# Rows of negated maxima: block turns on VectorE and small transfers in place of products on TensorE

## The chip, the cores and the metric

The kernel runs on one core of a Trainium2 chip. The metric is device time in microseconds (us), the median of several runs. The engines are called as in the profile: PE (TensorE, products; PEld is its loading of weights), DVE (VectorE), ACT (ScalarE), POOL (GpSimd) and SP (SyncE, which here only issues transfers). Each engine works through its own queue in order, and the queues wait for each other by semaphores.

## The reference

Two layers on x of shape (2, 256, 64, 64), all float32. The first is attention with 8 heads of 32 channels over 4096 positions, with a projection and the input added; the second is a non-local block over 1024 pooled positions.

```python
# layer 0
qkv = einsum('oc,bchw->bohw', w_qkv, x); q, k, v = split(qkv, 3, axis=1)   # 8 heads x 32
scores = einsum('bhdi,bhdj->bhij', q, k) / sqrt(32)
attn = softmax(scores, axis=-1)
out = einsum('bhij,bhdj->bhdi', attn, v)
x = einsum('oc,bchw->bohw', w_proj, out) + x
# layer 1
g_x = maxpool2(conv1x1(x, g_w, g_b));  theta_x = conv1x1(x[:, :64], theta_w, theta_b)
phi_x = maxpool2(conv1x1(x[:, 64:], phi_w, phi_b))
f = softmax(einsum('bnc,bcm->bnm', theta_x, phi_x), axis=-1)
y = einsum('bnm,bmc->bnc', f, g_x)
x = batchnorm(conv1x1(y, W_w, W_b)) + x
```

Both softmaxes subtract the maximum of each row (of each query) before the exponential. The change is about how these maxima get from one place to another.

## The kernel before

**Tiling.** An image (b, two of them) has two groups of four heads (`QUAD`, numbered n = 0 to 3 over both images). For each group, `attend` runs over 8 blocks of 512 queries (i), and in each block over 32 steps of 128 keys (j). A step has four score products (`score`, L491: heads 2 and 3 as `pair` 1, then heads 0 and 1), two exponentials on ACT (L675), the products with v of the step before (`weigh`, L518) and their addition on DVE (L528). The sums of the exponentials, for the softmax's denominators, go to POOL (`add`, L555) and to accumulating transfers that POOL issues (L544). The scores of one block stay in PSUM and each step adds the difference of two chunks of keys to them (`turn_kd`, `mid_kd`, `kd`, `last_kd`).

**Maxima.** The maximum of every query over all 4096 keys must be known before its block begins. `maxima(n, i)` computes them one block ahead, as a generator that `advance(maxes)` moves on twice a step: products of q and k into PSUM (`product`, L330; the four heads lie in four groups of 32 rows of PE), for heads 0 and 1 a maximum straight from PSUM (L342), for heads 2 and 3 in pairs, with a difference and a relu on ACT (L350) and one DVE operation for both (L357). When a block's maxima are complete, DVE reduces `part` to `neg`, 128 x 16 numbers with the queries on the partitions (L434).

**Rows.** The exponential wants minus the maximum added to scores in which the queries lie along the free axis. So `negate` (L146) splits `neg` on POOL into three bfloat16 terms whose sum is exact enough (L150 to L154) and lays them into a 128 x 512 tile, of which most is zero. `rows()` then multiplies the tile with an identity matrix, four products of 128 x 128 (L159), which turns it over, and ACT copies the result from PSUM (L170). `subtract` (L500) begins each block's scores with the product of ones and these rows (L503). `make_rows` (L453) is called at every even step and makes a block's rows at the second call after they are ready.

**Lead.** Before the loop over blocks, `first_block` computes the maxima of the first block in 33 slots, with the items (k, v and q of the first group, `make`) between them. After it, four v items are made with two `advance` after each, so the maxima are ahead of the blocks by 8 calls, which is four steps. `LEAD = 4` stands in the code and isn't used.

**Items.** In the first three groups each of the first seven blocks makes one chunk of k and v of the next group at step 30 (block 6 also at step 11), and most blocks a q at step 11. They take their x from one buffer, which SP loads.

**Layer 1** (`non_local`) does the same with 8 row blocks of 512 queries for each image. `maxima1` computes maxima (`most`, L862; `neg`, L868) ahead by six groups of 128 queries, `step` the scores of two chunks of keys with their exponential (L1009), `weigh` the products with the values. Its PE instructions keep the program's order (`product1`, L712). `ready[i + 1]()` makes the next block's rows at the start of the second half of block i. `result` divides: the denominators go over DVE, two small transfers (L953, L954), DVE, two more (L961, L964), and then DVE multiplies and adds (L968, L969) and SP stores z (L970).

**SP's queue** holds, in one order fixed at build time, the loads of x, the small transfers of the denominators (layer 0: L617, L619, L635, L637), the key differences that are put away and fetched (L271 to L291), and the stores of the result.

## Time and profile before

| | |
|---|---|
| median of 3 runs | 3787.51 us (3785.46 to 3788.95) |
| the profiled execution: time / span | 3789.17 us / 3787.1 us |
| granted PE clock | 0.998 |
| first block's subtraction (L503) starts | 90.5 us |
| layer 0 of image 0 / image 1, from that subtraction to the last block's end, about | 90 to 1690 us / 1949 to 3522 us |
| period of a block with k and v at its end / in the last group | 99.64 us / 96.13 us |
| period of the first block of the last group | 112.33 us |
| L159: products in layer 0 / layer 1, busy | 128, 12.5 us / 64, 6.2 us |
| L170: copies in layer 0 / layer 1, busy | 32, 19.1 us / 16, 9.4 us |

Busy time is what an engine spends on instructions; a line's idle time is how long its engine stood still just before it, with what ended the wait. The order of time lists a start, a duration, the engine (PE, DVE, SPq for SP's queue), the line and operation, the tiles as output<-input, the shape and how many were merged. The long period in the last group has one cause: DVE waits 12.8 us for weights of layer 1 that land late (L763, then L767), and PE waits for DVE.

### The profile page before, as it was taken

Reading aid. Unit: us, or ns where it says so; the run is one execution under the profiler, and the core shown is the slowest. Engines: PE = TensorE matmul, PEld = TensorE weight load, DVE = VectorE, ACT = ScalarE, POOL = GpSimd, SP = SyncE. Lnnn points to the kernel's source line nnn. Section 1 sums busy time; section 2 is a strip of 40 time slices with the busy share of each in tenths; the row PEclk is TensorE's granted clock in tenths of the full one; section 3 lists DMA queues with packets and bytes.
Section 4 is the critical chain, followed back from the end, with each engine's and each line's share of the span. In section 5 each row is a group of like instructions: output and inputs, shape, how many; then the busy total and the mean of one; then the engine's idle time right before and its main releaser. Section 6 shows DMA issues by size and latency. Waiting matters only on the chain.

```text
span 3787.1 us, 69847 instructions
## 1 busy us (share of the span) xinstructions
PE 3759.5 (99%) x27186; PEld 1250.3 (33%) x27186; DVE 2981.3 (79%) x5841; ACT 2701.0 (71%) x3383; POOL 3077.8 (81%) x1944
## 2 busy tenths in 40 slices
PE   9999999999999999999999999999989999999999
PEld 4323333333333333334433333333222223222343
DVE  5888888888888888884468888888878888895444
ACT  5888788778888878771247887887868888887222
POOL 1889999899999999892458999999989999997244
PEclk9999999999999999999999999999999999999999
DMA  1788888889888888892128888888888888889501
GB/s 59 151 171 172 175 171 175 172 169 195 174 172 171 173 173 177 179 192 43 29 68 165 173 175 181 172 182 172 173 169 175 174 173 173 174 170 186 100 18 45
DMA packets 136028, 578.56 MB, mean 153 GB/s; under 512 B 37904, under 2 KB 42000, under 8 KB 74512
## 3 DMA queue, kind: packets, MB, share of 16 engines
q0 software_dynamic: 73184, 509.64, 67.9%
q1 hardware_dynamic: 61824, 64.20, 5.7%
q8 instruction: 212, 3.47, 0.4%
q14 instruction: 120, 0.98, 0.1%
q10 hardware_dynamic: 688, 0.27, 0.0%
HBM read 59.09 MB, written 12.69 MB: 19 GB/s over the span
## 4 chain that ended last, share of the span: by engine, by line
PE 97%; DMA 1%; DVE 1%; ACT 0%; issue 0%; POOL 0%; SPq 0%; ACTq 0%; POOLq 0%; DVEq 0%
PE ps L330 29%; PE w L518 26%; PE s L491 23%; PE y L712 6%; PE f L712 3%; PE q L206 2%; PE v L194 2%; PE proj L712 1%; PE k L206 1%; PE g L712 1%; PE tp L712 1%; DMA r<-flat 0%; DMA flat<-r 0%; PE s L503 0%; PE wg L712 0%
## 5 line engine op out<-in xcount | busy, mean ns | idle before, releaser
L555 POOL TENSOR_TENSOR p<-p,p 128x1024 f32<-128x1024 f32 x945 | 2357.7, 2495 | 279.5 <-ACT p L675 262.1
L675 ACT ACTIVATE p<-s 128x1024 f32<-128x1024 f32 x2048 | 2101.1, 1028 | 582.3 <-PE s L491 574.6
L330 PE MATMUL ps<-k,q 32*128 32x512 f32 x6080 | 2037.7, 625 | 2.8 <-DVE part L342 1.2
L342 DVE TENSOR_REDUCE part<-ps 128x1 f32<-128x512 f32 x1984 | 1278.5, 686 | 369.7 <-PE s L491 343.8
L518 PE MATMUL w<-p,v 128*32 128x512 f32 x8192 | 1080.6, 604 | 1.2 <-ACT p L675 0.8
L330 PEld LDWEIGHTS ps<-k,q 32*128 32x128 f32 x6080 | 607.1, 183 | 805.5 <-DVE part L342 696.4
L491 PE MATMUL s<-q,mid_kd 32*128 32x512 f32 x3072 | 749.8, 614 | 0.0
L357 DVE CUSTOM_DVE_ANT_0 ps<-ps,over 128x512 f32<-128x512 f32 x1056 | 727.7, 692 | 26.7 <-PE ps L330 13.5
L528 DVE TENSOR_TENSOR y<-y,w 128x512 f32<-128x512 f32 x938 | 645.0, 688 | 98.4 <-PE w L518 97.2
L350 ACT ACTIVATE over<-ps 128x512 f32<-128x512 f32 x992 | 588.0, 593 | 16.2 <-PE ps L330 16.0
L330 PE MATMUL ps<-kd,q 32*128 32x512 f32 x1056 | 523.7, 592 | 12.2 <-DVE part L357 11.8
L491 PE MATMUL s<-q,kd 32*128 32x512 f32 x2048 | 507.8, 618 | 0.3 <-ACT p L675 0.3
L491 PE MATMUL s<-q,last_kd 32*128 32x512 f32 x2048 | 504.6, 614 | 1.2 <-ACT p L675 1.2
L330 PE MATMUL ps<-last_kd,q 32*128 32x512 f32 x960 | 472.5, 589 | 0.0
L518 PEld LDWEIGHTS w<-p,v 128*32 128x32 f32 x8192 | 166.7, 108 | 771.0 <-DVE part L342 708.7
L544 POOL DMA_DIRECT2D p<-p x448 | 394.1, 880 | 7.1 <-ACT p L675 4.5
L491 PEld LDWEIGHTS s<-q,mid_kd 32*128 32x128 f32 x3072 | 247.6, 183 | 189.5 <-ACT p L675 181.5
L712 PE MATMUL y<-p,kv 128*128 128x512 f32 x512 | 229.7, 599 | 0.0
L491 PEld LDWEIGHTS s<-q,kd 32*128 32x128 f32 x2048 | 166.0, 184 | 131.6 <-ACT p L675 128.9
L491 PEld LDWEIGHTS s<-q,last_kd 32*128 32x128 f32 x2048 | 167.2, 183 | 124.5 <-ACT p L675 108.0
L862 DVE TENSOR_REDUCE most<-f 128x1 f32<-128x512 f32 x128 | 79.5, 683 | 143.1 <-PE f L712 142.7
L886 POOL TENSOR_TENSOR sums<-sums,p 128x512 f32<-128x512 f32 x96 | 128.0, 1334 | 77.7 <-ACT p L1009 72.9
(136 smaller groups left out, 2738.0 us busy)
## 6 DMA issues: line engine op xcount, KB each, us to landing
p<-p POOLq DMA_DIRECT2D x478, 1024.0 KB, 7.8
x_q<-in_x_dram SPq DMA_DIRECT2D x30, 512.0 KB, 6.7
x_k<-in_x_dram SPq DMA_DIRECT2D x24, 512.0 KB, 5.9
y<-in_x_dram POOLq DMA_DIRECT2D x16, 512.0 KB, 6.3
r<-flat SPq DMA_DIRECT2D x120, 64.0 KB, 5.6
out_dram<-z SPq DMA_DIRECT2D x14, 512.0 KB, 2.8
x<-in_x_dram SPq DMA_DIRECT2D x7, 512.0 KB, 7.0
r<-flat SPq DMA_DIRECT2D x12, 256.0 KB, 3.5
```

What stands on the lines that cost most here:

```text
L330: nc.tensor.matmul(ps, q[n, i][bass.ts(h, D), bass.ts(g, P)], keys[bass.ts(h, D), :], start=True, stop=True,)
L342: reduced = nc.vector.tensor_reduce(part[:, g, h, j : j + 1], ps, AX.X, ALU.max)
L350: cut = nc.scalar.activation(over, ps, AF.Relu)
L357: reduced = nc.vector.tensor_tensor_reduce(out=ps, in0=ps, in1=over, scale=1.0, scalar=LEAST, op0=ALU.add, op1=ALU.max, accum_out=part[:, ...
L491: nc.tensor.matmul(s[:, t, :], kj[bass.ts(h, D), :], q[blk.n, blk.i][bass.ts(h, D), :], start=False, stop=True, skip_group_check=j > 0,)
L518: nc.tensor.matmul(w[bass.ts(h, D), :], v[blk.n][:, keys(one), h, :], p[h // 2][:, h % 2, :], start=at == 0, stop=at == len(steps) - 1,)
L528: summed = nc.vector.tensor_add(blk.num, blk.num, w)
L544: sent = nc.gpsimd.dma_start(out=blk.sums[n], in_=two, accum_op=ALU.add)
L555: added = nc.gpsimd.tensor_add(blk.sums[0], blk.sums[0], p[0])
L675: nc.scalar.activation(p[pair], s, AF.Exp, scale=scale)
L712: last1 = tc.keep_in_program_order(nc.tensor.matmul(*args, **kw))
L886: nc.gpsimd.tensor_add(acc[i][NC], acc[i][NC], p[:, j, :])
```

## The change

The identity matrix and the products with it go. The three terms of `neg` are laid into a narrower tile, 128 x 64, in such an order that turning each 32 x 32 block over puts the numbers of one query group along a row. DVE turns the blocks in one operation (`transpose`). Four transfers store the used rows into DRAM (`flat4`), in an order in which each of the 12 rows (three terms of four heads) is contiguous, and four more load them, three rows each, into a constant tile with zeros elsewhere (`kept`, one for each layer). All eight are issued by SP, and the loads wait for the stores.

The maxima are six steps ahead in place of four (`LEAD = 6`): four more `advance` calls stand before the loop. The rows are made at step 26 of each block, behind that step's addition on DVE (`summed`). The addition of step 25's exponentials on POOL (`late`) is issued behind the splits (`split`). `fetch` issues the load of x for step 30's items at step 22. Before the loop, one more v item stands among the slots, each item is made in two parts with an `advance` between, and the last three v items use the scores' PSUM buffers (`wide`).

In layer 1 the first rows are made after the values of block 6, the others in the second half of the block before, behind the latest maxima on DVE (`reduced1`).

```diff
-    ident = work.tile([P, P], F32, tag="r", name="ident", bufs=1)
-    make_identity(nc, ident)
-    ident_b = const.tile([P, P], BF16, name="ident_b")
-    nc.vector.tensor_copy(ident_b, ident)
...
-    t = const.tile([P, NB // P, QH, D], BF16, name="terms")
-    nc.gpsimd.memset(t, 0.0)
+    TERMS, BLOCKS = 3, NB // P // 2
+    terms = const.tile([P, BLOCKS, D], BF16, name="terms")
+    nc.gpsimd.memset(terms, 0.0)
+    kept = [const.tile([P, NB], BF16, name=f"rows{layer}") for layer in range(2)]
+    for t in kept:
+        nc.gpsimd.memset(t, 0.0)
 
     def negate(name, neg, layer=0):
...
-        nc.gpsimd.tensor_copy(t[:, :, :, 0], neg)
-        nc.gpsimd.tensor_sub(rest, neg, t[:, :, :, 0])
-        nc.gpsimd.tensor_copy(t[:, :, :, 1], rest)
-        nc.gpsimd.tensor_sub(rest, rest, t[:, :, :, 1])
-        nc.gpsimd.tensor_copy(t[:, :, :, 2], rest)
-
-        def rows():
-            pt = scratch(f"pt_{name}")
-            for j in range(NB // P):
-                nc.tensor.matmul(
-                    pt[:, bass.ts(j, P)],
-                    t[:, j].rearrange("p h d -> p (h d)"),
-                    ident_b,
-                    start=True,
-                    stop=True,
+        nonlocal split
+        at = [four(terms[:, :, a * QH * BLOCKS : (a + 1) * QH * BLOCKS]) for a in range(TERMS)]
+        neg = neg.rearrange("p (i l) h -> p l h i", l=BLOCKS)
...
+        nc.gpsimd.tensor_copy(at[0], neg)
+        nc.gpsimd.tensor_sub(rest, neg, at[0])
+        nc.gpsimd.tensor_copy(at[1], rest)
+        nc.gpsimd.tensor_sub(rest, rest, at[1])
+        split = nc.gpsimd.tensor_copy(at[2], rest)
+
+        def rows(behind=None):
+            to = kept[layer]
+            turned = work.tile([P, BLOCKS, D], BF16, tag="turned", name=f"turned_{name}", bufs=1)
+            with tc.issue_after(behind.ins) if behind else ExitStack():
+                nc.vector.transpose(
+                    turned.rearrange("p l c -> p (l c)"), terms.rearrange("p l c -> p (l c)")
                 )
-            if layer == 0:
-                to = work.tile([P, NB], BF16, tag="rows", name=f"rows_{name}", bufs=1)
-            else:
-                to = work.tile([P, 2, NB], BF16, tag="over", name=f"rows_{name}")[:, 0, :]
-            nc.scalar.copy(to, pt)
+            used = TERMS * QH * BLOCKS
+            flat = spare.tile([used, BLOCKS, P // D, D], BF16, tag="flat4", name=f"flat4_{name}")
+            for a in range(P // D):
+                nc.sync.dma_start(out=flat[:, :, a, :], in_=turned[a * D : a * D + used])
+            those = flat.rearrange("(t h i) l a c -> t h (i l a c)", t=TERMS, h=QH)
+            for h in range(QH):
+                nc.sync.dma_start(out=to[h * D : h * D + TERMS], in_=those[:, h])
             return to
...
-        pq = scratch(name)
+        pq = scores(name)[:, 0, :] if wide else scratch(name)
...
                             if pair == 1:
                                 advance(maxes)
+                                if j == NJ - LEAD:
+                                    with tc.issue_after(split.ins):
+                                        add(*late)
                             score(s, pair, blk, j)
...
-                    add(blk, j, p, two)
+                    if j == NJ - LEAD:
+                        make_rows(summed)
+                    if j == NJ - LEAD - 1:
+                        late = blk, j, p, two
+                    else:
+                        add(blk, j, p, two)
...
-                    if j % 2 == 0:
-                        make_rows()
+                    if j == NJ - 10:
+                        for item in present(items.get(NJ - 2, ())):
+                            fetch(*item)
...
         for i in range(NI):
             values(i)
+            if i == NI - 2:
+                rows = ready[0](reduced1[0])
...
-                if u > 0 and i + 1 < NI:
-                    with tc.issue_after(last1.ins):
-                        rows = ready[i + 1]()
                 two = [step(i, u)]
-                if NB // P * i + u + LEAD1 < NI * NB // P:
-                    advance(maxes1, 2)
-                elif waiting:
+                more = NB // P * i + u + LEAD1 < NI * NB // P
+                for a in range(2):
+                    if more:
+                        advance(maxes1)
+                    if u > 0 and i + 1 < NI and a == 0:
+                        rows = ready[i + 1](reduced1[0])
+                if not more and waiting:
...
-    LEAD = 4
+    LEAD = 6
...
+    items.append(("v", NI - 4))
     for n, (what, i) in enumerate(items):
-        advance(make(what, 0, i), 3)
-        to = slots * (n + 1) // len(items)
-        advance(maxes, to - gone)
-        gone = to
-    for i in range(NI - 4, NI):
-        advance(make("v", 0, i), 3)
-        advance(maxes, 2)
-        if i < NI - 2:
-            make_rows()
+        item = make(what, 0, i)
+        advance(item)
+        if n > 0:
+            advance(maxes)
+            gone += 1
+        advance(item, 2)
+        to = (slots - 1) * (n + 1) // (len(items) - 1) if n < len(items) - 1 else slots + 1
+        advance(maxes, to - 1 - gone)
+        gone = to - 1
+    for i in range(NI - 3, NI):
+        advance(make("v", 0, i, True), 3)
+        if i == NI - 2:
+            make_rows(reduced)
+        advance(maxes, 3)
+    advance(maxes, 3)
```

In the order in which the changed program stands on SP, the four loads of a block's rows in layer 0 follow straight on its four stores; in layer 1 the store of z (L970 before, L986 after) stands between them for row blocks 3 to 6 of each image, and for row block 2 the first small transfer of a result.

More of the change, by code (lines that the diff above doesn't have):

```diff
@@ L7 @@
 from concourse._compat import with_exitstack
-from concourse.masks import make_identity
 F32 = mybir.dt.float32
@@ L138, in keep_bn_rows @@
             )
-    t = const.tile([P, NB // P, QH, D], BF16, name="terms")
-    nc.gpsimd.memset(t, 0.0)
-    def negate(name, neg, layer=0):
-        rest = work.tile([P, NB // P, QH], F32, tag="rest", name=f"rest_{name}")
-        nc.gpsimd.tensor_copy(t[:, :, :, 0], neg)
-        nc.gpsimd.tensor_sub(rest, neg, t[:, :, :, 0])
-        nc.gpsimd.tensor_copy(t[:, :, :, 1], rest)
-        nc.gpsimd.tensor_sub(rest, rest, t[:, :, :, 1])
-        nc.gpsimd.tensor_copy(t[:, :, :, 2], rest)
-        def rows():
-            pt = scratch(f"pt_{name}")
-            for j in range(NB // P):
-                nc.tensor.matmul(
-                    pt[:, bass.ts(j, P)],
-                    t[:, j].rearrange("p h d -> p (h d)"),
-                    ident_b,
-                    start=True,
-                    stop=True,
-                )
-            if layer == 0:
-                to = work.tile([P, NB], BF16, tag="rows", name=f"rows_{name}", bufs=1)
-            else:
-                to = work.tile([P, 2, NB], BF16, tag="over", name=f"rows_{name}")[:, 0, :]
-            nc.scalar.copy(to, pt)
+    TERMS, BLOCKS = 3, NB // P // 2
@@ new lines, in conv_attention, with four @@
+    terms = const.tile([P, BLOCKS, D], BF16, name="terms")
[3 more added lines that the diff above has]
+        nc.gpsimd.memset(t, 0.0)
+    def negate(name, neg, layer=0):
+        def four(ap):
+            return ap.rearrange("p l (h i) -> p l h i", i=BLOCKS)
+        nonlocal split
+        at = [four(terms[:, :, a * QH * BLOCKS : (a + 1) * QH * BLOCKS]) for a in range(TERMS)]
+        neg = neg.rearrange("p (i l) h -> p l h i", l=BLOCKS)
+        rest = work.tile([P, BLOCKS, QH * BLOCKS], F32, tag="rest", name=f"rest_{name}")
+        rest = four(rest)
+        nc.gpsimd.tensor_copy(at[0], neg)
[9 more added lines that the diff above has]
+                    turned.rearrange("p l c -> p (l c)"), terms.rearrange("p l c -> p (l c)")
+                )
+            used = TERMS * QH * BLOCKS
[5 more added lines that the diff above has]
+                nc.sync.dma_start(out=to[h * D : h * D + TERMS], in_=those[:, h])
@@ L171, in rows @@
             return to
         return rows
+    split = None
     QUAD = [(b, qd) for b in range(B) for qd in range(QUADS)]
@@ L178, in conv_attention, with fetch @@
     held = {}
-    def make(what, n, i):
-        b, qd = QUAD[n]
+    def fetch(what, n, i):
+        b = QUAD[n][0]
         if (b, i) not in held:
@@ L185, in make @@
             held[b, i] = load_x(b, i, xs.tile([P, NC, NB], F32, tag="x", name=name))
+    def make(what, n, i, wide=False):
+        b, qd = QUAD[n]
+        fetch(what, n, i)
         xc = held[b, i]
         name = f"{what}_{b}_{qd}_{i}"
-        pq = scratch(name)
+        pq = scores(name)[:, 0, :] if wide else scratch(name)
         if what == "v":
@@ L449, in advance, with make_rows @@
             next(steps, None)
-    seen = set()
-    def make_rows():
+    def make_rows(behind=None):
         for i, r in enumerate(rows):
             if callable(r):
-                if i in seen:
-                    rows[i] = r()
-                seen.add(i)
+                rows[i] = r(behind)
     def attend(b, y):
@@ L796, in non_local @@
         nc.gpsimd.tensor_sub(dphi, phi[:, 2 * P :], phi[:, : M - 2 * P])
+        reduced1 = [None]
         def values(i):
@@ L809, in values @@
                     )
-                nc.vector.tensor_reduce(
+                reduced1[0] = nc.vector.tensor_reduce(
                     g[:, o, small].rearrange("p (r w) -> p r w", w=WW // 2),
@@ L833, in w_values @@
                 nc.vector.tensor_add(wg[:, 2 * t + j, :], a[:, bass.ts(j, C)], shift_row)
-        ready, reduced1 = [], [None]
+        ready = []
         LEAD1 = NB // P + 2
@@ L1019, in non_local @@
                 w_values(i // 2 - 1)
-        with tc.issue_after(last1.ins):
-            rows = ready[0]()
         for i in range(NI):
             for u in range(0, last + 1, 2):
-                if u > 0 and i + 1 < NI:
-                    with tc.issue_after(last1.ins):
-                        rows = ready[i + 1]()
                 two = [step(i, u)]
-                if NB // P * i + u + LEAD1 < NI * NB // P:
-                    advance(maxes1, 2)
-                elif waiting:
+                more = NB // P * i + u + LEAD1 < NI * NB // P
[5 more added lines that the diff above has]
+                if not more and waiting:
                     weigh(*waiting.pop(0))
```

## The prediction

> **What bounds the kernel now.** I read the page's busy times and its chain first, then the groups by form, then the order of time around one place of each stage that the change touches.

> ```profile
> PE 3759.5 (99%) x27186; PEld 1250.3 (33%) x27186; DVE 2981.3 (79%) x5841; ACT 2701.0 (71%) x3383; POOL 3077.8 (81%) x1944
> PE 97%; DMA 1%; DVE 1%; ACT 0%; issue 0%; POOL 0%; SPq 0%; ACTq 0%; POOLq 0%; DVEq 0%
> ```

> TensorE (PE) holds 97% of the chain, so a microsecond off PE's queue counts in full, and so does one that PE waits. A busy share with modelled ends doesn't prove this, so I looked at the pace. Here is the end of a block of layer 0 (last head group, image 1), PE's rows and the copy on ACT:

> ```profile
> 3239.29 1.07 PE L518 MATMUL w<-p,v 128*32 128x512 f32 x8
> 3242.22 1.06 PE L518 MATMUL w<-p,v 128*32 128x512 f32 x8
> 3243.22 0.40 PE L159 MATMUL pt<-ident_b,terms 128*128 128x128 bf16 x4
> 3243.84 0.61 ACT L170 CAST rows<-pt 128x512 bf16<-128x512 f32 x1
> 3245.55 1.07 PE L518 MATMUL w<-p,v 128*32 128x512 f32 x8
> 3246.55 0.39 PE L503 MATMUL s<-rows,ones_b 32*128 32x512 bf16 x2
> ```

> From one `w` to the next a step takes 2.93 us, in this block after block; the step that holds the four L159 products takes 3.33. So the old way costs PE 0.40 us a block. The L170 copy is beside it: ACT idles before most of its work.

> VectorE (DVE) works 2 x 0.645 + 0.69 + 0.14 + 0.69 = 2.81 us of a step's 2.93 (L342, L357 with its read, L528), so it has little room. The block period (99.64 us with new k and v, 96.13 in the last head group) varies by at most 0.25 in the blocks between: there PE waits for nobody.

> **What is removed.** Layer 0: L159 in 32 rows, one of them ahead of the loop: 31 x 0.40 = -12.4 us. Layer 1: in the order of time the four products start at 1824.18 and the next work at 1824.50: 16 x 0.32 = -5.1. Before row 1 of each image PE waits 0.86 us for POOL's last split (L154): 2 x 0.86 = -1.7, as the splits leave PE's queue. ACT's 48 copies and the identity's building were hidden: nothing.

> **What is added on DVE and POOL.** 48 transposes of 128x64 bf16. Nearest is L634, 64x32 f32, 196 ns; bounds 0.16 (a small DVE operation, L131) and 0.44 (L605). At 0.2 us a block it fits in what DVE has free, 0.1 us a step and gaps of some 4 us at the k and v items; if that cover went it would be 48 x 0.2 = 10 us. The transpose must not wait for POOL: the splits take 1.8 us (L150 to L154) and stand now before the addition of p25 instead of behind that of p27. In the trace POOL ends the addition of p26 0.1 to 0.7 us before the L434 reduction ends, so two steps earlier it is ready likewise; the splits end 1.9 us after the reduction, the transpose comes a step later, 2.65 us after it. It waits for nothing, with 0.7 to spare. POOL gives up some 0.7 us a block to the wait for L434 and gets it back at its idle time of 1.7 to 4.6 us at each block's start.

> **What is added on SP: a chain of two hops.** Eight transfers a row: four into DRAM, a wait for their landing, four back into `kept`. They are on the path only if they land after PE wants them. The rows that price them:

> ```profile
> 3224.59 4.12 SPq L637 DMA_DIRECT2D r<-flat  x4
> flat<-r SPq DMA_DIRECT2D x42, 8.0 KB, 4.8
> r<-flat SPq DMA_DIRECT2D x120, 64.0 KB, 5.6
> r<-flat SPq DMA_DIRECT2D x12, 8.0 KB, 1.6
> ```

> The first line is the nearest: four in a row on SP, into few partitions, under layer 0's load. Their issues start at 0, 0.4, 1.6 and 2.9 us. At the start of the program seven loads of x go out in a row at 0.46 each; these are my two ends, 1.35 and 2.9 us to the last issue. Landing in layer 0: L635 3.6 at least, 5.1 median; L637 2.9 and 5.6. I take 4.4 us for each hop and the slow issue: transpose at 2.9 us behind the reduction's end, last store issued at 5.8, landed 10.2, last load issued 13.1, landed 17.5. Quickest: 2.9 + 1.35 + 3.6 + 1.35 + 2.9 = 12.1. Slowest, with medians: 19.4.

> PE's need: the reduction's end to L503 is 14.60 us now in the 21 blocks with k and v at the end, 11.10 at the three changes of head group and in six blocks of the last, 9.47 before the last block. Two steps of lead add 5.86 (5.2 before the last block, whose steps run at 2.39 and 2.83), less 0.40: 20.1, 16.6 and 14.3. So at 17.5 nothing waits in 21 blocks; 6 x 0.9 = 5.4 us in the last head group; 3.2 at the last block; at two changes of group (the third is covered by layer 1) `turn_kd` and `mid_kd`, 448 KB, go out just ahead on the same queue, an estimated 2 us more: 2 x 3 = 6. Sum +15 us, ends 0 and +33. What stands behind the rows on SP (`mid_kd`, `last_kd`, the next x) is issued some 6 us later and needed 11 us or more after the block's start: nothing.

> [...]

> **Layer 1** is where I expect the loss. The second half of row block 3, image 0:

> ```profile
> 1824.50 1.13 PE L712 MATMUL f<-theta,kv 64*128 64x512 f32 x4
> 1828.94 2.80 DVE L968 TENSOR_TENSOR z<-z,r 128x512 f32<-128x512 f32 x2
> 1831.66 2.35 DVE L969 TENSOR_TENSOR z<-z,y 128x512 f32<-128x512 f32 x2
> 1834.03 0.40 SPq L970 DMA_DIRECT2D out_dram<-z  x1
> 1834.65 0.33 SPq L953 DMA_DIRECT2D flat<-r  x1
> 1836.16 0.38 PE L712 MATMUL f<-rows_l,ones_b 64*128 64x512 bf16 x2
> ```

> Count from T = 1824.50. The transpose follows the first two `most` reductions (T+3.5). In the changed program's order SP then has the four stores, and for rows 3 to 6 of each image the store of z *before* the four loads. That store waits for L969: T+9.5 now, 9.7 with the transpose. The loads follow 0.62 us behind it (as L953 does), from 10.4 to 11.7, and land at 1.6 us at 13.3; PE wants them at 11.66. So PE waits 1.7 us with the quick issue, 4.0 with the slow one; I take 2.2, nearer to the quick end, since here SP's queue is almost empty and the nearest landing is 1.6. 8 x 2.2 = +17.6 (11.6 to 32). Behind the loads stands L953 of the next result, about 2 us later; its r still lands before z needs it. Rows 1, 2 and 7 have no such store ahead: stores land T+7.2, loads T+10.2, no wait (1.6 us each by the slow issue, +10 in the upper end).

> **Ahead of the loop.** Two more steps of maxima (1.9 us each between the v items at 85.6) come before the loop; at the end two steps run without products, 0.3 us less each: +3.2. The items in halves: DVE is starved behind each whole item.

> ```profile
> 24.28 0.70 DVE L357 CUSTOM_DVE_ANT_0 ps<-ps,over 128x512 f32<-128x512 f32 x1 [1.54 <-ACT k L220]
> 30.23 0.70 DVE L357 CUSTOM_DVE_ANT_0 ps<-ps,over 128x512 f32<-128x512 f32 x1 [1.31 <-PE ps L330]
> ```

> An item is 1.9 us of PE; cut in two, each piece starves DVE by at most 1.4 - 0.95 = 0.45, so 0.5 of 1.4 us is won an item: 13 x 0.4 = -5 (0 to -13: no gain, or DVE never dry, when PE's own work there becomes the bound). Together -2. The x load brought forward only keeps it ahead of the rows on SP.

> **Sum**, against the profiled span of 3787.1 us (that run 3789.2; median of the runs 3787.5): -12.4 - 6.8 - 2 + 15 + 17.6 = +11.4. On the median: 3799 us.

> **Rivals.**
> - *The rows are in time (faster).* If both hops land at L635's and L637's least times with quick issues, layer 0 waits nowhere, layer 1 only its 1.7: -12.4 - 6.8 - 2 + 0 + 13.6 = -7.6; with twice the gain of the halves -13: 3775. For it: L635's and L637's bytes are more than these rows have. Against: 4 issues at 1.2 us are the rule for L637. It decides from a chain under 14.3 us in layer 0.
> - *Even.* Chain at 16.5 us, 4 us of waits in layer 0, 14 in layer 1: -3, 3785.
> - *SP's slow issue everywhere (slower still).* Slow ends in both layers: -12.4 - 6.8 + 25 + 40 - 2 = +44: 3831. For it: L758 to L763 take 1.1 to 1.35 each too. Against: layer 1's queue is idle.

> **Chances.** Forecast 0.42 (own range 3789 to 3814); in time 0.26; even 0.16; slow issue 0.16. The low end is the second case's better gain with some more, 3770; the high end leaves out half of the last: 3828. Faster by over 0.2% (7.6 us, about what the runs can tell from no change) 0.27; within 0.23 (the even case and the forecast's lower edge); slower 0.50.

> **What would show it.** No L159 in the groups; steps of 2.93 us to the block's end; waits of PE before the subtraction put down to a DMA, none in blocks with k and v, 1 to 3 us in the last head group; in layer 1, PE idle before the `rows` product for rows 3 to 6, and there the loads issued right behind L986's store. It is wrong if four issues on SP in layer 0 end within 1.5 us, if PE waits in blocks with k and v (chain over 20 us), or if the DVE transpose waits for POOL and PE's step with it.

## The result, and the profile after

The changed kernel takes 3813.56 us (median of four runs, 3808.93 to 3817.24), the kernel before 3787.02 in the same series: a ratio of 1.0071, with a 95% interval of 1.0057 to 1.0084. It is slower by about 26.5 us. The profiled execution took 3816.07 us with a span of 3814.3, so its comparison with the span before (3787.1) has 27.2 us to explain.

The page of the changed kernel, its busy times and its chain:

```profile
PE 3768.9 (99%) x26994; PEld 1244.3 (33%) x26994; DVE 2992.6 (78%) x5888; ACT 2679.1 (70%) x3335; POOL 3079.5 (81%) x1944
PE 89%; DMA 3%; POOL 3%; issue 2%; DVE 2%; ACT 1%; SPq 1%; POOLq 0%; DVEq 0%; ACTq 0%
```

PE issues 192 products fewer and is still "busy" 9 us longer, in part because it runs part of the time at a lower clock (a mean of 0.994, before 0.998; below). The chain says more: PE held 97% of it and now holds 89%. PE waits for others, for POOL and for transfers above all.

The order of time at the end of a block of the last head group (image 1, the same block as was shown of before):

```profile
3248.32 0.28 DVE L444 TENSOR_REDUCE neg<-part 128x16 f32<-128x128 f32 x1
3251.24 0.24 DVE L166 STREAM_TRANSPOSE turned<-terms 128x64 bf16<-128x64 bf16 x1
3251.51 4.83 SPq L172 DMA_DIRECT2D flat<-turned  x4
3255.36 1.06 PE L523 MATMUL w<-p,v 128*32 128x512 f32 x8
3258.29 1.06 PE L523 MATMUL w<-p,v 128*32 128x512 f32 x8
3258.97 3.58 SPq L175 DMA_DIRECT2D rows<-flat  x4
3261.22 1.07 PE L523 MATMUL w<-p,v 128*32 128x512 f32 x8
3264.14 1.07 PE L523 MATMUL w<-p,v 128*32 128x512 f32 x8
3265.14 0.39 PE L508 MATMUL s<-rows,ones_b 32*128 32x512 bf16 x2
```

The products of L159 are gone, every step takes 2.93 us to the block's end, and the subtraction (L508, once L503) follows the last `w` after 1.00 us, as it did: here the rows come in time. An undisturbed block takes 99.29 us instead of 99.64. So this part of the change works, and the loss is elsewhere. The stretches from one block's first subtraction to the next, from PE's start times in both traces, show where:

```
stretch                                before    after   after - before
start of the program to block 0         90.49    92.19    +1.70
block 7  (last of head group 0)         96.22   103.23    +7.01
block 8  (first of head group 1)       101.15   104.65    +3.50
block 15 to layer 1's first rows       182.67   187.63    +4.96
layer 1, image 0, to block 16          174.02   176.84    +2.82
block 23 (last of head group 2)         96.40   102.49    +6.09
block 30                                92.85    95.11    +2.26
block 31 to layer 1's first rows       171.36   175.33    +3.97
layer 1, image 1, to the last product  173.52   176.20    +2.68
the other 26 blocks together                              -7.8
```

The three stretches at the ends of head groups 0, 1 and 2 hold 18.1 of the 27.2 us, and no step of the prediction has them. In the order of time there, the changed kernel:

```profile
824.96 2.48 POOL L246 TENSOR_TENSOR first_kd<-k 128x512 f32<-128x512 f32 x2
826.27 1.22 PE L340 MATMUL ps<-first_kd,q 32*128 32x512 f32 x1 [2.94 <-POOL first_kd L246]
827.28 1.06 PE L340 MATMUL ps<-first_kd,q 32*128 32x512 f32 x1
```

and the kernel before:

```profile
824.77 2.50 POOL L236 TENSOR_TENSOR first_kd<-k 128x512 f32<-128x512 f32 x2
828.42 0.60 PE L330 MATMUL ps<-first_kd,q 32*128 32x512 f32 x1
```

POOL makes `first_kd`, the key differences that the next head group's maxima read, at step 8 of the last block (`before_all`), as before. Its first half was ready at 826.0 and wanted at 828.4. With maxima six steps ahead PE wants it two steps, 5.86 us, sooner. The 2.4 us to spare become a gap of 3.5 us between two starts of PE, 2.94 of them idle. The busy times and the clock around it (columns: stretch, its length, busy time and count of each engine, granted PE clock, share of the DMA engines, GB/s), the changed kernel:

```profile
811.00:822.70 11.70, 11.70 (x86) 4.00 (x80) 8.20 (x17) 8.39 (x12) 11.62 (x8) 1.00 0.64 130
822.70:826.30 3.60, 0.66 (x6) 0.03 (x2) 1.09 (x2) 0.93 (x1) 3.60 (x3) 0.96 0.81 164
826.30:832.00 5.70, 5.70 (x20) 1.54 (x24) 1.80 (x4) 1.51 (x2) 3.88 (x3) 0.50 0.63 128
```

and the kernel before in the last of these stretches:

```profile
826.30:832.00 5.70, 5.70 (x52) 1.76 (x48) 5.70 (x13) 4.65 (x7) 5.62 (x4) 1.00 0.68 138
```

In the 5.7 us after the wait PE starts 20 products where it started 52: the granted clock is 0.50. The wait is paid for about twice, once as idle time and once as products at half the clock.

### The profile page after: what moved, and what is told of

It reads as the page before. It is cut to its first block, busy times and chain, and to the rows that moved or that the text cites. A ratio compares the mean times of both kernels' runs of the same rounds, so it can differ in the third digit from the quotient of the medians.

```text
span 3814.3 us, 70045 instructions
## 1 busy us (share of the span) xinstructions
PE 3768.9 (99%) x26994; PEld 1244.3 (33%) x26994; DVE 2992.6 (78%) x5888; ACT 2679.1 (70%) x3335; POOL 3079.5 (81%) x1944
## 4 chain that ended last, share of the span: by engine, by line
PE 89%; DMA 3%; POOL 3%; issue 2%; DVE 2%; ACT 1%; SPq 1%; POOLq 0%; DVEq 0%; ACTq 0%
PE ps L340 27%; PE w L523 24%; PE s L496 21%; PE y L726 4%; PE f L726 3%; DMA p<-p 2%; POOL p L560 2%; PE proj L726 1%; PE k L216 1%; PE q L216 1%; PE g L726 1%; PE v L204 1%; PE tp L726 1%; DVE z L984 0%; DMA rows<-flat_l 0%
## 5 line engine op out<-in xcount | busy, mean ns | idle before, releaser
L340 PE MATMUL ps<-kd,q 32*128 32x512 f32 x1056 | 525.3, 593 | 11.6 <-DVE part L367 10.6
L1025 ACT ACTIVATE p<-f 128x1024 f32<-128x1024 f32 x64 | 65.5, 1023 | 263.7 <-PE f L726 263.7
```

The costliest lines, as they stand in the source:

```text
L340: nc.tensor.matmul(ps, q[n, i][bass.ts(h, D), bass.ts(g, P)], keys[bass.ts(h, D), :], start=True, stop=True,)
```

## The experiments

Twelve kernels ran, each against the kernel before on the same chip. Ratios are to that kernel (its medians were 3786.7 to 3787.5), with 95% intervals.

**1. The wait for `first_kd`.** POOL's work and the q item that stands ahead of it are moved two steps forward, by as much as the maxima moved.

```diff
-        return {7: [("q", n + 1, 1)]}
+        return {5: [("q", n + 1, 1)]}
...
-                        if (i, j) == (NI - 1, 8) and blk.n + 1 < len(QUAD):
+                        if (i, j) == (NI - 1, 6) and blk.n + 1 < len(QUAD):
```

> The changed kernel with only this altered: in the last block of a head group the q item stands at step 5 instead of 7, and the differences of the next group's keys (`first_kd`, on POOL) are made at step 6 instead of 8. Theory (the lead of six steps brings the products that read `first_kd` two steps forward, while POOL still makes it at step 8): the three gaps of PE at 822.7, 1630.1 and 2697.2 (3.1 to 3.5 us each) go, and with them the 5.7 us at a granted clock of 0.50 behind each (some 2.9 us each): 3 x 6.3 = 19 us less, 3795 (3791 to 3799), and block 7 falls from 103.2 to about 97. Rival (PE stalls there because the rows' transfers slow POOL's accumulating DMAs, and `first_kd` is only what the wait is put down to): the gaps stay or move by a step, 3808 or more.

3798.16 us, ratio 1.0027 (1.0017 to 1.0037): 15.4 us less than the changed kernel. All three gaps (3.1 to 3.5 us between two starts of PE) are gone, block 7 takes 96.62, block 23 96.21, block 15's stretch 182.17. In this kernel's order of time and busy times:

```profile
820.90 2.74 POOL L246 TENSOR_TENSOR first_kd<-k 128x512 f32<-128x512 f32 x2
824.10 0.66 PE L340 MATMUL ps<-first_kd,q 32*128 32x512 f32 x1
826.30:832.00 5.70, 5.70 (x48) 1.62 (x48) 5.70 (x11) 4.59 (x7) 5.62 (x4) 1.00 0.95 191
```

The theory holds and the rival falls. The three stretches give back 18.3 us; the profiled run of this kernel loses 2.2 of that in block 0, where it shows a granted clock of 0.50 from 91.3 to 98.1 us, behind the short gaps ahead of the loop, and the changed kernel's profiled run doesn't.

**2. Is it the lead or the rows' transfers?** The kernel before with the lead alone: PE still turns the rows, no new transfer.

```diff
-    LEAD = 4
+    LEAD = 6
...
         advance(make("v", 0, i), 3)
-        advance(maxes, 2)
+        advance(maxes, 3)
```

> The kernel before with only the lead changed: maxima six steps ahead instead of four (three steps behind each of the last four v items instead of two), the rows still turned by PE, no new transfers. Theory (the lead alone brings the wait for `first_kd`): the same three gaps of PE of 3.1 to 3.5 us in blocks 7, 15 and 23, which then take some 102.5, 362 and 102.5 us; with the two later steps ahead of the loop 3787.5 + 18 + 4 = 3810 (3803 to 3814). Rival (the gaps come from the rows' transfers): blocks 7, 15 and 23 as before (96.2, 356.7, 96.4), 3791. Also looked at: block 8 and block 31, which became 3.5 and 6.7 us longer. If POOL's earlier splits or the lead are their cause, they are as long here; if the rows' transfers on SP are, block 8 is 101 here and block 31 345.

3813.75 us, ratio 1.0068 (1.0055 to 1.008): the lead alone costs as much as the whole change. Block 7 takes 102.77, block 15's stretch 189.18, block 23 101.50, with the same wait:

```profile
831.66 2.49 POOL L236 TENSOR_TENSOR first_kd<-k 128x512 f32<-128x512 f32 x2
832.98 1.22 PE L330 MATMUL ps<-first_kd,q 32*128 32x512 f32 x1 [2.51 <-POOL first_kd L236]
```

Block 8 is 101.21 here, as before, so what happens there comes with the rest of the change, not with the lead. Block 31's stretch is 174.82, nearly the 175.33 of the changed kernel, with the lead alone. And block 0 starts at 98.4 us: ahead of the loop the lead costs 7.9 us, not the 3.2 of the prediction.

**3. The halves.** The changed kernel with whole items ahead of the loop.

```diff
-        item = make(what, 0, i)
-        advance(item)
+        advance(make(what, 0, i), 3)
         if n > 0:
             advance(maxes)
             gone += 1
-        advance(item, 2)
```

> The changed kernel with only this altered: ahead of the loop the attention items are made whole, with all the maxima behind each item, instead of in halves. Theory of the prediction (each half starves VectorE less): the first block begins 5 us later than its 92.2 us (0 to 13 later), so 3819. Rival (PE's own work sets the pace there, the halves give nothing): the first block begins within 1 us of 92.2 and the time is 3814.

3817.59 us, ratio 1.0075 (1.0061 to 1.0088), 4.0 more than the changed kernel. The medians alone don't tell that from none (the two intervals overlap), but block 0 starts at 95.57 instead of 92.19, and the seven kernels here with the changed kernel's code ahead of the loop start it between 92.1 and 92.8: the halves are worth some 3.4 us, close to the 5 of the prediction.

**4. How long is the rows' way?** The changed kernel with the lead of before, so that PE waits for the rows everywhere and the wait shows the way's length.

```diff
-    LEAD = 6
+    LEAD = 4
...
-        advance(maxes, 3)
-    advance(maxes, 3)
+        advance(maxes, 2)
+    advance(maxes, 2)
```

> The changed kernel with only the lead put back to four steps (two steps of maxima behind the last v items). The prediction's step that is tested: the way of the rows takes 17.5 us from the reduction's end, and PE needs them after 14.2 us in blocks with k and v and 10.7 in the last head group (9.1 before the last block). If it takes 17, PE now waits before every block: 21 x 2.8 + 8 x 6.3 + 7.9 = some 117 us, with the lower granted clock behind each wait more, less the 18 us of the three gaps at `first_kd`: 3900 to 3990. Rival (the way is short, 12.1 us, the prediction's quick end): no wait in the blocks with k and v, 1.4 us in the last head group, 3800. The waits before the subtraction give the way's length in each block.

3888.17 us in its one run, below the 3900 to 3990 that a way of 17 us would have given: PE waits in all blocks but the first of each image, 79 us in all beyond the usual 0.5 between two of its starts. A block of the last head group, in the order of time:

```profile
2895.84 0.28 DVE L444 TENSOR_REDUCE neg<-part 128x16 f32<-128x128 f32 x1
2898.76 0.24 DVE L166 STREAM_TRANSPOSE turned<-terms 128x64 bf16<-128x64 bf16 x1
2899.03 5.06 SPq L172 DMA_DIRECT2D flat<-turned  x4
2905.80 1.06 PE L523 MATMUL w<-p,v 128*32 128x512 f32 x8
2906.21 3.55 SPq L175 DMA_DIRECT2D rows<-flat  x4
2911.45 0.75 PE L508 MATMUL s<-rows,ones_b 32*128 32x512 bf16 x2 [4.58 <-DMA rows<-flat]
```

From the reduction's end (2896.12) to the product that waited is 15.3 us, and in the other blocks 14.8 to 17.7. That is shorter than the 17.5 of the prediction, longer than the rival's 12.1, and otherwise divided: SP needs 5.06 us to issue four stores and 3.55 for four loads, and the landings follow 2.1 and 1.7 us after the last issue has ended. A lead of four steps doesn't cover this way, and 8.6 of its 15.3 us are issuing. Block 0 starts at 87.55 here, so in the changed kernel the two steps of lead cost 4.6 us ahead of the loop.

**5. Layer 1.** The changed kernel with the store of z behind the four loads on SP's queue.

```diff
+                loaded = nc.sync.dma_start(out=to[h * D : h * D + TERMS], in_=those[:, h])
-                nc.sync.dma_start(out=to[h * D : h * D + TERMS], in_=those[:, h])
...
-            nc.sync.dma_start(out=dst[:, :, cols], in_=z)
+            with tc.issue_after(loaded.ins):
+                nc.sync.dma_start(out=dst[:, :, cols], in_=z)
```

> The changed kernel with only this altered: in layer 1 the store of z is put on SP's queue behind the four loads of the rows. Theory (the loads stand behind a store that waits for the last operation on z): a row block with such a store takes 22.9 us now and the one without 21.6, so 8 x 1.3 = 10 us less, 3803 (3801 to 3806), all row blocks between 21.5 and 21.8, and PE's gaps of 1.4 us before the rows' product fall to 0.5. Rival (the chain of stores and loads itself is too long there, whatever stands between): the row blocks stay over 22.5 and the time over 3810.

3802.14 us, ratio 1.0037 (1.0024 to 1.005): 11.4 less than the changed kernel, where 10 were expected. The order of time of row block 3 of image 0, first the changed kernel:

```profile
1839.52 3.24 SPq L172 DMA_DIRECT2D flat_l<-turned_l  x4
1843.16 2.35 DVE L985 TENSOR_TENSOR z<-z,y 128x512 f32<-128x512 f32 x2
1845.54 0.41 SPq L986 DMA_DIRECT2D out_dram<-z  x1
1846.14 1.60 SPq L175 DMA_DIRECT2D rows<-flat_l  x4
1848.68 0.73 PE L726 MATMUL f<-rows,ones_b 64*128 64x512 bf16 x2 [0.84 <-DMA rows<-flat_l]
```

then the kernel with the store behind the loads:

```profile
1838.30 3.24 SPq L172 DMA_DIRECT2D flat_l<-turned_l  x4
1842.87 1.20 SPq L176 DMA_DIRECT2D rows<-flat_l  x4
1844.60 0.41 SPq L988 DMA_DIRECT2D out_dram<-z  x1
1846.45 0.38 PE L727 MATMUL f<-rows,ones_b 64*128 64x512 bf16 x2
```

In the first, the loads stand ready to go behind a store that waits for DVE's last addition. In the second they leave as soon as the stores have landed, and PE waits for nothing. All inner row blocks take 21.61 us (in the changed kernel the four with a store ahead 22.6 to 23.0, in the kernel before 21.84), and each image's layer 1 is 2.6 us shorter than before the change.

**6. Both together.** The edits of experiments 1 and 5.

> The changed kernel with the two corrections together: `first_kd` and the q item two steps earlier, and in layer 1 the store of z behind the rows' loads. Theory (two separate waits, both gone): the sum of what each gave alone, -15.4 and -11.5, so 3813.6 - 26.9 = 3786.7 (3784 to 3790), even with the kernel before. Rival (one gives back what the other gained): over 3793.

3784.40 us, ratio 0.9995 (0.9986 to 1.0004): the two gains add up, and the change, so mended, is even with the kernel before.

**7. Block 8.** At a change of head group four copies of key differences (`mid_kd`, `last_kd`) stand behind the rows on SP. The order of time of the changed kernel:

```profile
890.60 3.33 SPq L175 DMA_DIRECT2D rows<-flat  x4
893.97 0.35 SPq L292 DMA_DIRECT2D mid_kd<-away  x1
894.36 0.54 SPq L298 DMA_DIRECT2D last_kd<-first_kd  x1
894.95 1.14 SPq L292 DMA_DIRECT2D mid_kd<-away  x1
896.13 1.26 SPq L301 DMA_DIRECT2D last_kd<-first_kd  x1
910.78 0.86 POOL L568 DMA_DIRECT2D p<-p  x1 [5.46 <-DMA p<-p]
918.92 1.02 ACT L683 ACTIVATE p<-s 128x1024 f32<-128x1024 f32 x1 [3.38 <-DMA p<-p]
```

They go out within 2.2 us (before: over 6 us, the last at 888.4), then POOL waits for its accumulating transfer, ACT for a p buffer, and PE has a gap of 2.15 us at 918.3, with 3.4 us at a granted clock of 0.50 behind it. Three kernels took the copies out of this place. The first issues all of them on ACT's queue (`nc.scalar.dma_start` in `renew`):

> The changed kernel with only this altered: the copies of the key differences at a change of head group (`mid_kd`, `turn_kd`, `last_kd`) are issued on ACT's queue instead of SP's. Theory (on SP they are held up behind the rows' four loads and then go out together, at 894 to 896 us, beside POOL's accumulating DMA, so that ACT waits for a p buffer and PE for ACT): the gap of PE at 918.3 goes and block 8 falls from 104.6 to about 101: 3.5 us less, 3810. Rival (POOL itself is late at the start of block 8, since it now waits for the reduction or takes the splits earlier): block 8 stays at 104 to 105 and the time at 3813. A third, against both: the issues cost ACT more than they give back, 3816 or more.

3823.12 us, ratio 1.0093 (1.008 to 1.0107). Block 8 falls to 99.53 and its gap is gone, as the theory says, but blocks 7 and 23 and the stretch of block 15 lose 5.7 to 5.8 us each: the third expectation. ACT's instructions there:

```profile
889.71 0.33 ACTq L292 DMA_DIRECT2D mid_kd<-away  x1
890.08 0.60 ACT L360 ACTIVATE over<-ps 128x512 f32<-128x512 f32 x1 [3.53 <-DMA flat<-turned]
```

The copy makes ACT stand still for 3.5 us, by the profile for a landing, and with it the exponentials that PE needs. The other two kernels stay on SP, with both corrections, and put the rows' loads behind the second copy of `mid_kd`, and then behind the first of `last_kd` as well:

```diff
+                        if j == NJ - 4 and held_loads:
+                            with tc.issue_after(copied.ins):
+                                held_loads.pop()()
```

> As the kernel with both corrections, and at a change of head group the rows' four loads stand behind the second copy of `mid_kd` on SP's queue, which needn't wait for the stores to land. Theory (that copy, held up behind the loads, goes out together with three others beside POOL's accumulating DMA, and ACT then waits for its p buffer): block 8 falls from 102.7 to 104.6 to about 101 and the gap of PE some 22 us after its start goes, 2 to 4 us less than the kernel with both corrections. Rival (the three other copies, which go out then in any case, or POOL's order): block 8 stays over 102.5, no difference.

> The changed kernel with both corrections (3784.4), and at a change of head group the rows' four loads stand behind the second copy of `mid_kd` and behind the first copy of `last_kd` on SP's queue, so that only the third of `mid_kd` and the second of `last_kd` are left to go out behind them. Theory (copies that go out together behind the loads delay POOL's accumulating DMA and then ACT's p buffer): block 8 falls from 102.0 to 102.9 (as it was with one copy moved) to 101 or less, 1 to 2 us less for block 8, perhaps as much for block 24. Rival (the order of the copies doesn't decide; the rows' own transfers there do): block 8 stays at 102 to 103.

3784.26 us (0.9994; 0.9986 to 1.0003) and 3785.25 (0.9994; 0.9985 to 1.0003): no difference from experiment 6. Block 8 takes 102.91 and 101.67 (experiment 6: 102.01), and in the second kernel the rows themselves come late to block 8 (a gap of PE of 2.98 us at 887.0, block 7 98.42). So the order of these copies behind the loads doesn't decide by itself. Block 8 is as it was with the lead alone (experiment 2); what the rest of the change does there, by its transfers' own work or by what they hold up, stays open. Part of its size is the clock: experiment 5, whose layer 0 is the changed kernel's, takes 102.03 there, with a gap of 1.62 us and no low clock behind it, experiment 1 takes 102.67 without the low clock, and experiment 3, which has it, 104.21. So it is 1 to 2 us over the kernel before where the low clock stays away, whether `first_kd` is mended or not.

**8. What layer 1 gives alone.** The kernel before, layer 0 untouched, with the new rows only in layer 1 and the store behind the loads (the rows' tile is cleared on POOL for each row block, for lack of room for a constant one).

> The kernel before with the new rows in layer 1 alone (VectorE's transpose, the eight transfers, and the store of z behind the four loads); layer 0 with lead four, PE's products and whole items as before. Theory (layer 1's part is a gain once the store is out of the way): 21.6 us a row block instead of 21.84 and 2.6 us less for each image, 3787.2 - 5.2 = 3782 (3780 to 3784), so that all of the layer 0 part, with its first correction, is worth about -3 + 5 = +2. Rival (layer 1 gains only because layer 0's lead leaves it in another state): no difference from before, 3787.

3784.48 us, ratio 0.9996 (0.9987 to 1.0006), 2.5 more than the expected 3782 and just outside its range. In its trace layer 1 is 2.6 us shorter for each image (171.43 and 170.90), as it is in experiment 6; what the median lacks isn't in layer 1, but such a small difference isn't told from none. It is the time of experiment 6: the whole layer 0 part, even with `first_kd` mended, brings nothing that these runs can tell.

**9. The wait that both kernels have.** In block 24 DVE waits for the row of scales and PE for DVE, before the change and after it. The two products are put behind the attention's last sum:

```diff
-            nc.vector.tensor_mul(ww_sb[:, c, :], ww_sb[:, c, :], scale_row)
+            with tc.issue_after(newest[0].ins):
+                nc.vector.tensor_mul(ww_sb[:, c, :], ww_sb[:, c, :], scale_row)
```

> The kernel before with one thing changed that the change doesn't touch: VectorE's two products of the second image's layer 1 weights with the row of scales (L767) stand behind the last sum of the attention loop, no longer in block 24, where VectorE waits 12.8 us for the row of scales and PE 12.4 us for VectorE. Theory (that wait alone makes block 24 112.3 us long): the gap at 2757 goes, with the 6.5 us at a granted clock of 0.51 behind it, block 24 takes 98 to 101 and the time is 3787.2 - 13 = 3774 (3771 to 3778). Rival (ACT and POOL wait for the accumulating DMA there in any case, POOL 5.34 us before L563): a gap of some 5 us stays, 3780.

3777.45 us, ratio 0.9973 (0.9965 to 0.9982). Block 24 takes 101.37 instead of 112.33. In the busy times of this kernel PE works through most of the place where it stood still for 12 us. The kernel before:

```profile
2757.00:2769.50 12.50, 0.73 (x4) 0.00 (x0) 1.44 (x5) 1.02 (x1) 3.60 (x3) 0.71 0.98 227
2769.50:2776.00 6.50, 6.46 (x24) 2.24 (x28) 3.17 (x6) 1.51 (x2) 2.34 (x1) 0.51 0.32 66
```

and this kernel:

```profile
2757.00:2769.50 12.50, 11.12 (x84) 3.18 (x77) 9.36 (x17) 7.99 (x10) 5.99 (x4) 1.00 0.90 214
2769.50:2776.00 6.50, 5.70 (x44) 1.69 (x40) 4.73 (x9) 3.88 (x6) 6.34 (x5) 1.00 0.55 111
```

Two gaps of 2.0 and 1.4 us remain. The gain, 9.3 us of the 13 expected, is inside the theory's range at its weak end; the rival's gap of some 5 us isn't there. With layer 1's new rows as well:

> The kernel before with both: the new rows in layer 1 alone with the store of z behind the loads, and VectorE's two products behind the attention loop. Theory: two separate places, so the sum of what each gives alone, 3787.2 - 5.2 - 13 = 3769 (3765 to 3774). Rival (one hides the other): no better than the better of the two.

3773.86 us, ratio 0.9965 (0.9953 to 0.9978): the fastest kernel of the study, 13 us below the kernel before and 40 below the changed one. Block 24 takes 98.09 here, with one gap of 1.4 us left. Nearly three quarters of the gain over before has nothing to do with the change.

## Why the prediction was right, and where it was not

It gave 3799 us, within 3770 to 3828, and slower as the likeliest; 3813.56 is slower, within the range, and at the upper edge of the forecast's own 3789 to 3814. That the size is near is luck: the waits for the rows, +15 in the sum, came to 1.7, and a wait of 18 us that the sum doesn't have took their place. What it understood of the loss is layer 1's part, 10.7 of 26.5 us. With `first_kd` mended (experiment 1) the kernel takes 3798.16, almost the forecast's 3799, and this is luck too: blocks 8 and 31 and smaller things then hold what the forecast gave to the rows.

- *Products removed in layer 0, -12.4.* Right in kind, mis-sized: an undisturbed block with k and v is 0.35 us shorter, not 0.40, so 31 x 0.35 = -10.9.
- *Layer 1's products and POOL's last split, -6.8.* Experiment 5 shows what layer 1 is without waits: 2 x 2.6 = -5.2. An inner row block gains 0.23, not 0.32; the first, with the wait for POOL, 1.26 (predicted 1.18).
- *The transpose on DVE hidden.* Right: 0.24 us (estimated 0.2), at the place the prediction gave it, 2.64 us behind the reduction's end, and the steps stay at 2.93.
- *Lead and halves ahead of the loop, -2.* Wrong in sign: +1.7. The halves gave some 3.4 (the prediction's working has 0.5 an item and its sum takes 0.4); the lead cost 7.9 in the kernel before and 4.6 in the changed one, not 3.2.
- *Waits for the rows in layer 0, +15.* The needs were right (20.1 and 16.5 us measured against 20.1 and 16.6), the way was mis-sized: 15.3 us in the block shown in experiment 4 and 14.8 to 17.7 in all, where 17.5 was taken for every block. PE waits for rows before block 26 (0.4) and the last block (1.25) only, 1.7 us instead of 15. In experiment 4's block the last store starts 3.7 us after the first and the last load 2.5 (2.9 was taken for each), and after these starts it takes 3.4 and 2.7 us to go on (4.4 was taken): the landings were quicker. Of the 15.3 us, 8.6 were eight issues in a row on one queue; the landings took 2.1 and 1.7 us behind the end of the last issue.
- *Waits in layer 1, +17.6.* The mechanism, its eight places and its cause are as predicted (experiment 5). The size was 5.4 us an image, 10.7 in all: 1.3 a row block, not 2.2, and under the quick end of 1.7.
- *What stands behind the rows on SP: nothing.* Wrong. Block 8 is 3.5 us longer in the profiled execution, and not with the lead alone (experiment 2). The prediction looked only at when the copies are needed; what delays block 8 instead stays open (experiment 7).
- *The step that failed* is the sentence on the lead: it costed two more steps of maxima ahead of the loop and nothing behind it. Moving the maxima two steps forward moves all that they read, and `first_kd` had 2.4 us to spare for 5.86. That is 18 us, more than the whole sum of the forecast; experiments 1 and 2 show it from both sides. Both rows that tell it stood in the trace of before: POOL's L236 at 824.77 and the first product with it at 828.42.

With the terms as measured (-10.9 - 5.2 + 1.7 + 1.7 + 10.7) the change would have been at -2.0, too small to be told from nothing. Of the other 29.2 us, 19.1 are the three waits (18.1 and three blocks' 0.35), 3.9 block 8, and 4.3 block 31, where PE has a gap of 2.2 us behind POOL's and ACT's wait for an accumulating transfer; 1.9 are spread over the rest. Most of block 31's part is the clock: the kernel before has a gap of 1.74 us at the same place (3453.5), with no low clock behind it, and the three kernels of experiments 8 and 9, whose layer 0 has the old lead, have 1.55 to 2.83 us there with 3.4 or 6.8 us at 0.50 behind and take 173.0 to 176.3 us as well. Whether the change makes the low clock likelier there isn't shown.

## What to carry to other kernels

When work is moved forward in a schedule, list what each moved instruction reads and who makes it at what step, and compare each one's time to spare with the distance of the move. Four small transfers in a row cost their issuing queue more here (3.6 to 5.1 us) than the landing of the last (1.7 to 2.1), and what stands ahead of them in that queue, like a store that waits for its data, delays them too (by some 2 us a row block in layer 1). A gap in PE's work of some 3 us costs up to about twice its length here (with the one of 3.53 us, block 7 takes 7.0 us longer), so one such wait outweighs many small savings in the steady state.

## What the runs showed of the hardware

**A transfer on ACT's queue.** The copies, which hold up only other transfers while they wait on SP, stopped ACT for 3.5 us in experiment 7: here a queue with work of its own pays for a wait that a queue of transfers alone only passes on.
